# A graph network on one core: the zero fill, the attention table and the edge tables moved out of the preparation

## The chip, the cores and the metric

The kernel runs on one core of a Trainium2 chip. A core has a matrix engine (PE, whose weight loads are listed apart as PEld), a vector engine (DVE), an activation engine (ACT), GpSimd (POOL), and SyncE (SP), which here only issues transfers. Each engine takes its instructions in order from its own queue and waits at semaphores for the others. Transfers are issued from the queues of SP, ACT and POOL and carried by 16 DMA engines.

The metric is the device time of one execution in microseconds (us), as a median of several runs. Beside it stands one execution taken by the hardware profiler, with its span (first to last instruction).

## The reference

A graph of 12,500 nodes and 400,000 edges, sorted by destination; each node has 32 features. Four layers follow one another, each as `x = layernorm(x + layer(x))`:

```python
x = _layernorm(x + _L0_gnn_ref(x, src, dst, w1_W, w1_b, w2_W, w2_b, a))   # attention over the sources
x = _layernorm(x + _L1_gnn_ref(x, edge_index, 3))                         # three rounds of means
x = _layernorm(x + _L2_gnn_ref(x, edge_index, edge_attr_32, W1, b1, W2, b2))  # edge network, maximum
x = _layernorm(x + _L3_gnn_ref(x, edge_index))                            # three rounds of normed sums
```

L0 weighs the sources of a node by a softmax of `a . w2(x_dst - x_src)`. Within one destination the part of `x_dst` cancels, so each source has one weight, `exp(logit - maximum)`, which can be put into a table once. L1 and L3 sum the rows of the sources for each destination. L2 runs a small network over every edge and takes the maximum for each destination; it needs, edge by edge, the row of the source and the row of the destination.

## The kernel before

**A.** The kernel writes the graph down as a dense matrix A of small counts, one byte for each pair of nodes: 25 chunks of 512 destinations, each against 98 groups of 128 sources. Sums over edges then are matmuls of A with a table of node rows, split into three bf16 parts (`split`, `x3`).

**Preparation (lines 395 to 617).** `zero` is memset and written to all of `starts_d` (50 MB, line 429, on ACT's queue); it is needed in the edge layer. `code` and `srcs` (1.6 MB each) are loaded, a word is packed for each edge and stored to `code_d`. `firsts` holds the destination of every 128th edge. 25 comparisons (`mk`, line 460) with matmuls count them into `row`, which goes out to `row_d` and comes back as `row_i`; 25 gathers fetch these rows of `dst`, and `lt` and `ws` (lines 493 to 497) give the first edge of each window of four destinations. `ws` goes out to `ws_d`. Then comes `attention_table` (line 335): for each of 25 groups of four, PE transposes of `X`, an ACT copy to `xT`, matmuls with `wc`, and three DVE operations into `ex`, `lg` and `X`; at the end the extremes of `lg`, an exponential, a product over all of `ex` and `split` into `x3`. Then come the edge layer's tables (lines 504 to 560): in six pieces, `dsh` and `rw` are loaded, DVE makes `rows_d`, the flags `cont_d` (two stores) and the heads of three stages. Then `ws` is read back (line 567), counts and the list of overflowing windows are made (lines 563 to 617, 803 to 821).

**Build (lines 620 to 850).** Windows are the rows of a chunk. `runs(q)` says how many runs of 128 edges chunk q has for each of its 128 windows: 4, 3, 2 or 1. What does not fit goes to an extra chunk `Ax` of at most 128 rows of 512 edges, handled first (c = -1, four runs). For each chunk `chunk_keys` gathers the words `g` from `code_d`; `edge_keys` unpacks them (`ki`, line 643) to `pl`. `build_half` makes one-hots on DVE, `ol` (line 706) and `oh` (line 711), from the pool `hot`, one pair for each run in each of eight steps; PE multiplies them (line 721, `pa`), ACT copies to `at` (line 727), SP stores `at` to A (line 732). Between these matmuls `go_on(4)` takes steps from the list `steps`: generators that multiply a finished half by `x3` (`multiply`, line 741) and finish a chunk of the attention layer (`attend`).

**L1 (lines 879 to 906).** Three rounds of `R.product`: for each chunk SP loads A in two tiles `a` (line 314, three buffers), PE multiplies them (line 318), and DVE checks the counts with `top` (line 325), one quarter of A in each round. Then follow the edge layer and L3.

**Order.** A scheduler interleaves the instructions of each engine's queue when the program is built; it follows the data and the buffers, so code written later may stand earlier in a queue.

Of the kernel before, what the change touches and what calls it, by code (L numbers as in the profile page):

```python
# [8 lines left out]
F32 = mybir.dt.float32  # L9
F16 = mybir.dt.float16  # L10
BF16 = mybir.dt.bfloat16
# [11 lines left out]
P = 128  # L23
# [28 lines left out]
def runs(q):  # L52

    return 4 if q == 0 else 3 if q == 1 else 2 if q < 9 else 1
# [60 lines left out]
def dense_path(ctx, tc, bad_i, x, src, dst, edge_attr, w1T, w1_b, w2, w2T, w2_b, aT,  # L115
# [140 lines left out]
    class Rounds:  # L256
        def __init__(self, st, x3s=2):
            self.x3p = st.enter_context(tc.tile_pool(name="x3p", bufs=x3s))
            self.wk = st.enter_context(tc.tile_pool(name="wk", bufs=2))
            self.one = st.enter_context(tc.tile_pool(name="one", bufs=1))  # L260
# [72 lines left out]
    def attention_table(R, t0):  # L333

        lg = R.one.tile([P, H], F32, name="lg")
        x3 = R.new_x3()
        with tc.tile_pool(name="l0", bufs=1) as l0, \
                tc.tile_pool(name="l0p", bufs=1, space=PSUM) as l0p, \  # L340
                tc.tile_pool(name="l0y", bufs=3, space=PSUM) as l0y:
            pu = l0p.tile([P, P], F32, name="pu")
            nc.tensor.matmul(pu[:D, 0:1], w2_sb, a_sb, start=True, stop=True)
            nc.vector.memset(wc[D:, D:D + 1], 0.0)
            nc.vector.tensor_scalar_mul(wc[:D, D:D + 1], pu[:D, 0:1], -1.0)
            xT = [l0.tile([D + 1, 4, P], F32, name=f"xT{i}") for i in range(2)]
            for t in xT:
                nc.vector.memset(t[D:], 1.0)
            for n_, h0 in enumerate(range(0, H, 4)):
                k = min(4, H - h0)  # L350
                pT = l0y.tile([P, 4, P], F32, name="y")
                for j in range(k):
                    nc.tensor.transpose(pT[:D, j, :], X[:, h0 + j, :], ident)
                nc.scalar.copy(xT[n_ % 2][:D, :k], pT[:D, :k])
                pm = l0y.tile([P, 4, P], F32, name="y")
                for j in range(k):
                    nc.tensor.matmul(pm[:, j, :2 * D + 1], xT[n_ % 2][:, j, :], wc,
                                     start=True, stop=True)
                nc.vector.tensor_copy(t0[:, h0:h0 + k, :D], pm[:, :k, :D])
                nc.vector.tensor_copy(lg[:, h0:h0 + k], pm[:, :k, D])  # L360
                nc.vector.tensor_add(X[:, h0:h0 + k, :], X[:, h0:h0 + k, :],
                                     pm[:, :k, D + 1:2 * D + 1])

            mm = l0.tile([P, 2], F32, name="mm")
            nc.vector.reduce_max(mm[:, 0:1], lg, axis=AX.X)
            nc.vector.tensor_reduce(mm[:, 1:2], lg, axis=AX.X, op=OP.min)
            nc.vector.tensor_scalar_mul(mm[:, 1:2], mm[:, 1:2], -1.0)
            pu = l0p.tile([P, P], F32, name="pu")
            nc.tensor.transpose(pu[:2, :], mm, ident)
            ext = l0.tile([2, 1], F32, name="ext")  # L370
            nc.vector.reduce_max(ext, pu[:2, :], axis=AX.X)
            pick = l0.tile([2, 2], F32, name="pick")
            nc.vector.tensor_scalar(pick, ident[:2, :2], ext, None, op0=OP.mult)
            pu = l0p.tile([P, P], F32, name="pu")
            nc.tensor.matmul(pu[:, :2], ones[:2, :], pick, start=True, stop=True)
            gm = l0.tile([P, 2], F32, name="gm")
            nc.vector.tensor_copy(gm, pu[:, :2])
            wide = l0.tile([P, 1], F32, name="wide")
            nc.vector.tensor_add(wide, gm[:, 0:1], gm[:, 1:2])
            fits = l0.tile([P, 1], F32, name="fits")  # L380
            nc.vector.tensor_scalar(fits, wide, SPAN, None, op0=OP.is_le)
            nc.vector.tensor_sub(more, more, fits)
            nc.vector.tensor_scalar_add(more, more, 1.0)
            nc.vector.tensor_scalar_mul(gm, gm, -1.0)
            nc.scalar.activation(t0[:, :, D], lg, AF.Exp, bias=gm[:, 0:1])
            nc.vector.tensor_mul(t0[:, :, :D], t0[:, :, :D], over(t0[:, :, D], H))
            nc.vector.memset(t0[:, :, D + 1], 1.0)
            for h0 in range(0, H, 14):
                split(R.wk, x3, t0[:, h0:h0 + 14, :], h0, 14, F0)
        return x3  # L390
# [4 lines left out]
    with ExitStack() as build:  # L395
# [29 lines left out]
        with tc.tile_pool(name="prep", bufs=1) as prep, \  # L425
                tc.tile_pool(name="prep2", bufs=2) as prep2:
            zero = prep.tile([P, 25 * D], F32, name="zero")
            nc.vector.memset(zero, 0.0)
            nc.scalar.dma_start(starts_d[:E].rearrange("(p b t) d -> p b (t d)", p=P, t=25),
                                zero[:, None, :].to_broadcast([P, C // 25, 25 * D]))  # L430
# [59 lines left out]
            x3 = attention_table(R, ex)  # L490

# [10 lines left out]


        with tc.tile_pool(name="e_prep", bufs=2) as prep:
            CP = -(-C // 5)
            d0 = keys.tile([P, 1], F32, name="d0")
            run = keys.tile([P, 1], F32, name="run")
            for s in range(len(HS) + 1):
                e0, Cs = P * cuts[s], cuts[s + 1] - cuts[s]

                def view(ap):
                    return ap[e0:e0 + P * Cs].rearrange("(p t) -> p t", p=P)

                cont0, single, fix, first_row = heads[s]
                nc.gpsimd.iota(run, pattern=[[0, 1]], base=e0 - 1, channel_multiplier=Cs,
                               allow_small_or_imprecise_dtypes=True)
                pieces = -(-Cs // CP)
                size = -(-Cs // pieces)
                for c0 in range(0, Cs, size):
                    n = min(size, Cs - c0)  # L520
                    sl = slice(c0, c0 + n)
                    dsh = prep.tile([P, CP + 1], I32, name="dsh")[:, :n + 1]
                    if e0 or c0:
                        nc.sync.dma_start(dsh, bass.AP(tensor=dst.tensor,
                                                       offset=dst.offset + e0 + c0 - 1,
                                                       ap=[[Cs, P], [1, n + 1]]))
                    else:
                        nc.vector.memset(dsh[:, 0:1], -1)
                        nc.sync.dma_start(dsh[:, 1:], view(dst)[:, sl])
                        nc.sync.dma_start(dsh[1:, 0:1], bass.AP(tensor=dst.tensor,  # L530
                                                                offset=dst.offset + Cs - 1,
                                                                ap=[[Cs, P - 1], [1, 1]]))
                    rw = prep.tile([P, CP], I32, name="rw")[:, :n]
                    nc.sync.dma_start(rw, view(src)[:, sl])
                    lo = prep.tile([P, CP], I32, name="lo")[:, :n]
                    hi = prep.tile([P, CP], I32, name="hi")[:, :n]
                    table_row(rw, rw, lo, hi)
                    nc.sync.dma_start(view(rows_d)[:, sl], rw)
                    t = prep.tile([P, CP], F32, name="t")[:, :n]
                    acc = prep.tile([P, 1], F32, name="acc")  # L540
                    nc.vector.tensor_tensor(t, dsh[:, 1:], dsh[:, :n], op=OP.is_lt)
                    nc.vector.reduce_sum(acc, t, axis=AX.X)
                    nc.vector.tensor_add(more, more, acc)
                    cont = prep.tile([P, CP], F32, name="cont")[:, :n]
                    nc.vector.tensor_tensor(cont, dsh[:, 1:], dsh[:, :n], op=OP.is_equal)
                    nc.sync.dma_start(view(cont_d[0])[:, sl], cont)
                    contb = prep.tile([P, CP], F32, name="contb")[:, :n]
                    nc.vector.tensor_scalar(contb, cont, -0.5, BIG, op0=OP.add, op1=OP.mult)
                    nc.vector.tensor_scalar_mul(contb, contb, 2.0)
                    nc.sync.dma_start(view(cont_d[1])[:, sl], contb)  # L550
                    if c0 == 0:
                        nc.vector.tensor_copy(cont0, cont[:, 0:1])
                        nc.vector.tensor_copy(d0, dsh[:, 1:2])
                        table_row(first_row, dsh[:, 1:2], lo[:, 0:1], hi[:, 0:1])
                    nc.vector.tensor_scalar(t, dsh[:, 1:], d0, None, op0=OP.is_equal)
# [1407 lines left out]
```

## Time and profile before

| what | us |
|---|---|
| median of three runs (11362.96 to 11370.98) | 11369.12 |
| the profiled execution | 8876.0 |
| its span | 8873.8 |
| preparation, to the first one-hot `oh` | 352.9 |
| build of A with the attention layer, to the last product at 1681 | about 1330 |
| L1, from its first matmul at 1696.6 to about 3414 | about 1717 |
| edge layer, to about 7519 | about 4105 |
| L3, to the end | about 1355 |

The profiled execution is 2493 us shorter than the median of the runs; its mean granted PE clock is 0.785. Busy over the span: PE 87%, PEld 53%, DVE 51%, ACT 18%, POOL 37%. Such shares are means over stages that have different limits, so the stages are read one by one: a digit in the page's slices is the busy share of an engine in tenths, a timeline row gives when an instruction started and who ended the idle time before it.

### The profile page before, as it was taken

Reading aid. Unit: us, or ns where it says so; the run is one execution under the profiler, and the core shown is the slowest. Engines: PE = TensorE matmul, PEld = TensorE weight load, DVE = VectorE, ACT = ScalarE, POOL = GpSimd, SP = SyncE. Lnnn points to the kernel's source line nnn. Section 1 sums busy time; section 2 is a strip of 40 time slices with the busy share of each in tenths; the row PEclk is TensorE's granted clock in tenths of the full one; section 3 lists DMA queues with packets and bytes.
Section 4 is the critical chain, followed back from the end, with each engine's and each line's share of the span. In section 5 each row is a group of like instructions: output and inputs, shape, how many; then the busy total and the mean of one; then the engine's idle time right before and its main releaser. Section 6 shows DMA issues by size and latency. Waiting matters only on the chain.

```text
span 8873.8 us, 98544 instructions
## 1 busy us (share of the span) xinstructions
PE 7726.1 (87%) x38282; PEld 4718.2 (53%) x38282; DVE 4490.1 (51%) x9484; ACT 1623.5 (18%) x3211; POOL 3302.1 (37%) x3398
## 2 busy tenths in 40 slices
PE   2678899999999997688888888888869958999999
PEld 1468899755656554333433433443325635655655
DVE  2799988666666774333333333333333333366211
ACT  0224577400000001111111111111112211100000
POOL 1001110000000115777777777777777774000000
PEclk8689999999999997555555555555558969999999
DMA  7112244577777774222222122222226726777776
GB/s 273 49 60 112 119 172 176 232 286 286 284 290 286 292 292 148 57 54 55 51 54 57 50 56 54 53 54 52 56 52 201 249 69 204 266 289 286 283 288 240
DMA packets 442397, 1439.34 MB, mean 162 GB/s; under 512 B 115551, under 2 KB 200863, under 8 KB 428351
## 3 DMA queue, kind: packets, MB, share of 16 engines
q1 hardware_dynamic: 312864, 1317.77, 39.8%
q0 software_dynamic: 108576, 60.70, 4.1%
q10 hardware_dynamic: 20480, 54.47, 1.6%
q8 instruction: 304, 4.98, 0.2%
q14 instruction: 173, 1.42, 0.1%
HBM read 1155.20 MB, written 277.47 MB: 161 GB/s over the span
## 4 chain that ended last, share of the span: by engine, by line
PE 47%; POOL 27%; issue 9%; DVE 4%; DMA 3%; ACT 1%; POOLq 0%; ACTq 0%; DVEq 0%; SPq 0%
PE y L318 32%; POOL ef L105 26%; PE y L741 3%; PE y L987 3%; DMA ef<-table,rows 3%; DVE oh L711 2%; PE z L253 2%; PE pa L721 2%; DVE ol L706 1%; PE pv L1294 1%; PE ph L1276 1%; POOL ends L105 1%; PE pT L1247 1%; PE y L247 1%; PE ph L1278 1%
## 5 line engine op out<-in xcount | busy, mean ns | idle before, releaser
L105 POOL DMA_INDIRECT ef<-table,rows x3125 | 2953.3, 945 | 952.1 <-issue 922.9
L318 PE MATMUL y<-a,x 128*96 128x512 fp8e4 (+1 forms) x13338 | 2886.2, 376 | 21.7 <-DMA a<-Ax 21.7
L318 PEld LDWEIGHTS <-x 128*96 128x96 bf16 x13338 | 1627.4, 124 | 1161.0 <-issue 16.3
L1249 DVE COPY eT<-pT 96x512 f32<-96x512 f32 x782 | 535.8, 685 | 2362.2 <-PE pT L1247 2350.2
L325 DVE TENSOR_REDUCE top<-a 128x1 f32<-128x6272 uint8 x204 | 1363.6, 6685 | 658.0 <-DMA a<-A 636.4
L1247 PE MATMUL pT<-ident,ef 128*96 128x128 f32 x3125 | 1139.4, 411 | 518.3 <-DMA ef<-table,rows 489.5
L1247 PEld LDWEIGHTS pT<-ident,ef 128*96 128x96 f32 x3125 | 546.1, 186 | 1495.2 <-DMA ef<-table,rows 919.9
L1276 PE MATMUL ph<-eT,mw 96*64 96x256 f32 x1564 | 807.7, 616 | 91.2 <-DVE eT L1249 72.9
L1294 PE MATMUL pv<-mw,hT 128*128 128x64 f32 x3124 | 803.4, 398 | 89.8 <-ACT hT L1281 81.8
L1294 PEld LDWEIGHTS pv<-mw,hT 128*128 128x128 f32 x3124 | 695.3, 302 | 345.4 <-ACT hT L1281 202.2
L721 PE MATMUL pa<-oh,ol 128*128 128x196 bf16 x5184 | 715.8, 263 | 119.7 <-DVE oh L711 69.3
L1278 PE MATMUL ph<-eT,mw 96*64 96x256 f32 x1562 | 808.1, 617 | 0.0
L727 ACT ACTIVATE at<-pa 128x784 uint16<-128x784 f32 x816 | 651.2, 823 | 552.2 <-PE pa L721 527.9
L1281 ACT ACTIVATE hT<-ph,mb 128x256 f32<-128x256 f32 x781 | 370.5, 474 | 2072.8 <-PE ph L1278 2065.3
L741 PE MATMUL y<-at,x 128*102 128x256 fp8e4 x4998 | 724.6, 274 | 22.1 <-ACT at L727 22.1
L110 POOL DMA_INDIRECT starts_d<-X,start_i x98 | 95.0, 969 | 1645.0 <-DVE X L228 1622.5
L721 PEld LDWEIGHTS <-ol 128*128 128x128 bf16 x5184 | 544.2, 118 | 165.6 <-issue 108.7
L711 DVE TENSOR_TENSOR oh<-bins_h,pl 128x1568 bf16<-128x1568 bf16 x648 | 626.0, 966 | 0.0
L741 PEld LDWEIGHTS <-x 128*102 128x102 bf16 x4998 | 545.5, 126 | 40.1 <-issue 30.8
L706 DVE TENSOR_TENSOR ol<-la,lb 128x512 bf16<-128x512 bf16 x1296 | 491.1, 418 | 75.6 <-PE pa L721 75.1
L105 POOL DMA_INDIRECT g<-code_d,ws_i x25 | 119.0, 4760 | 1006.7 <-DVE ki L643 1006.7
L987 PE MATMUL y<-a,x 128*96 128x512 fp8e4 (+1 forms) x1950 | 492.5, 390 | 0.9 <-DVE x L241 0.9
(298 smaller groups left out, 4088.8 us busy)
## 6 DMA issues: line engine op xcount, KB each, us to landing
a<-A SPq DMA_DIRECT2D x240, 3136.0 KB
A<-at SPq DMA_DIRECT2D x98, 1568.0 KB
a<-A SPq DMA_DIRECT2D x48, 1152.0 KB
starts_d<-zero ACTq DMA_DIRECT2D x1, 50000.0 KB
ef<-table,rows POOLq DMA_INDIRECT x3125
attr<-in_edge_attr SPq DMA_DIRECT2D x63, 768.0 KB
begin<-starts_d SPq DMA_DIRECT2D x63, 768.0 KB
scan<-o SPq DMA_DIRECT2D x63, 768.0 KB
```

The source lines that it names most:

```text
L105: return nc.gpsimd.indirect_dma_start(out=o, out_offset=None, in_=tab, in_offset=IndirectOffsetOnAxis(ap=idx, axis=0))
L318: nc.tensor.matmul(y[:3 * F, :nq * Q], x3[:, h, :3 * F], a[:, :nq, h - h0, :], start=(h == first), stop=(c < 0 and h == H - 1))
L325: nc.vector.reduce_max(top[:, col:col + 1], a[:, quarter].bitcast(U8).rearrange("p h c -> p (h c)"), axis=AX.X)
L711: nc.vector.tensor_tensor(oh, bins_h[:, None].to_broadcast([P, 4, HJ, 2]), pairs(pl[:, t, 0, half * 64 + w0:half * 64 + w0 + 8])[:, :, Non ...
L721: nc.tensor.matmul(pa[:, 2 * b + i, :HJ], ols[t][:, u, :, :, 2 * b + i].rearrange("p a b -> p (a b)"), ohs[t][:, 2 * u + b, :, i], start=( ...
L727: nc.scalar.activation(at[:, qd, :, off:off + 8].rearrange("p h (w j) -> p h w j", w=4), pa[:, :, :HJ].rearrange("p w (h j) -> p h w j", h ...
L741: nc.tensor.matmul(y[:3 * F0, half * 2 * Q:(half + 1) * 2 * Q], x3[:, h, :3 * F0], at[:, :, h, :], start=(h == 0), stop=(c < 0 and h == H ...
L987: nc.tensor.matmul(y[:3 * D, :nq * Q], x3[:, h, :3 * D], a[:, :nq, h - h0, :], start=(h == lo), stop=(h == hi - 1))
L1247: nc.tensor.transpose(pT[:3 * D, j, :], B.ef[:, t + j, :], ident)
L1276: nc.tensor.matmul(ph[:HID, :ka], mw1, eT[:, :ka], start=True, stop=True)
L1278: nc.tensor.matmul(ph[HID:2 * HID, :k - 2], mw1, eT[:, 2:k], start=True, stop=True)
L1294: nc.tensor.matmul(pv[:, j].rearrange("p h d -> p (h d)"), hT[:, j, :], mw2, start=True, stop=True)
```

## The change

- The zero fill is no longer first. `zero` is made from the first keys (`pl` of the extra chunk, times 0.0), and the store to `starts_d` is issued on ACT's queue after them.
- `attention_table` becomes the generator `attention`, put first on `steps`, so that its parts are taken by `go_on` in the build of the extra chunk. Its PSUM tiles come from the build's pools `p_y` (two buffers) and `p_z`, its `xT` from `ys`. The product over `ex` is made in seven parts. `multiply` takes its PSUM tile when it begins.
- The edge layer's tables become the function `edge_tables`, called after L1's first round.
- The pool `hot` has five buffers for each of `ol` and `oh` instead of six.
- `runs(q)` is 2 up to q = 6 instead of q = 8.

```diff
-    return 4 if q == 0 else 3 if q == 1 else 2 if q < 9 else 1
+    return 4 if q == 0 else 3 if q == 1 else 2 if q < 7 else 1
...
-    def attention_table(R, t0):
...
+    def attention(x3, t0, lg, p_y, p_z):
...
+        def part2(n_, h0, k):
+            pm = p_y.tile([P, CH], F32, name="y0").rearrange("p (k e) -> p k e", e=P)
+            for j in range(k):
+                nc.tensor.matmul(pm[:, j, :2 * D + 1], xT[n_ % 2][:D + 1, j, :], wc,
+                                 start=True, stop=True)
+            late.append((h0, k, pm))
+
+        def part3(h0, k, pm):
+            nc.vector.tensor_copy(t0[:, h0:h0 + k, :D], pm[:, :k, :D])
+            nc.vector.tensor_copy(lg[:, h0:h0 + k], pm[:, :k, D])
+            nc.vector.tensor_add(X[:, h0:h0 + k, :], X[:, h0:h0 + k, :],
+                                 pm[:, :k, D + 1:2 * D + 1])
+
+        for n_, h0 in enumerate(range(0, H, 4)):
+            k = min(4, H - h0)
+            pT = p_y.tile([P, CH], F32, name="y0").rearrange("p (k e) -> p k e", e=P)
+            for j in range(k):
+                nc.tensor.transpose(pT[:D, j, :], X[:, h0 + j, :], ident)
+            nc.scalar.copy(xT[n_ % 2][:D, :k], pT[:D, :k])
+            yield
+            part2(n_, h0, k)
+            yield
+            yield
+            part3(*late.pop(0))
+            yield
...
+        for h0 in range(0, H, 14):
+            sl = slice(h0, h0 + 14)
+            nc.vector.tensor_mul(t0[:, sl, :D], t0[:, sl, :D], over(t0[:, sl, D], 14))
+            nc.vector.memset(t0[:, sl, D + 1], 1.0)
+            split(wk, x3, t0[:, sl, :], h0, 14, F0)
+            yield
+
+    def edge_tables():
...
-            zero = prep.tile([P, 25 * D], F32, name="zero")
-            nc.vector.memset(zero, 0.0)
-            nc.scalar.dma_start(starts_d[:E].rearrange("(p b t) d -> p b (t d)", p=P, t=25),
-                                zero[:, None, :].to_broadcast([P, C // 25, 25 * D]))
...
-            x3 = attention_table(R, ex)
...
-        hot = build.enter_context(tc.tile_pool(name="hot", bufs=6))
+        hot = build.enter_context(tc.tile_pool(name="hot", bufs=5))
...
+        x3 = R.new_x3()
+        lg = keys.tile([P, H], F32, name="lg")
...
         def multiply(at, y, c, half, last, done):
+            if half == 0:
+                y.append(p_y.tile([P, CH], F32, name="y0"))
+            y = y[0]
...
+        nc.vector.tensor_scalar_mul(
+            zero.bitcast(BF16), todo[0][0].rearrange("p t m w -> p (t m w)")[:, :2 * 25 * D], 0.0)
+        nc.scalar.dma_start(starts_d[:E].rearrange("(p b t) d -> p b (t d)", p=P, t=25),
+                            zero[:, None, :].to_broadcast([P, C // 25, 25 * D]))
...
+        steps.append(attention(x3, ex, lg, p_y, p_z))
         for c in range(-1, NQ):
             pl, n, to, halves, done = todo.pop(0)
-            y = p_y.tile([P, CH], F32, name="y0")
+            y = []
...
             R.product(x3, post1, r)
+            if r == 0:
+                edge_tables()
```

## The prediction

> **What bounds the kernel now.** I read first the page's forty slices, each about 222 us wide:
>
> ```profile
> PE   2678899999999997688888888888869958999999
> DVE  2799988666666774333333333333333333366211
> PEclk8689999999999997555555555555558969999999
> DMA  7112244577777774222222122222226726777776
> ```
>
> No engine is full in slices 0 and 1, the preparation. Slices 1 to 7 build A, 7 to 15 are L1, 15 to 33 the edge layer, 33 to 39 L3. The change touches the preparation, the build and the start of L1, so the timeline of the first 360 us comes next (start, duration, engine, line, operation; in brackets the idle time before it and who ended it):
>
> ```profile
> 2.43 0.65 ACTq L429 DMA_DIRECT2D starts_d<-zero  x1
> 4.68 34.95 SPq L434 DMA_DIRECT2D code<-in_dst  x1
> 86.89 0.18 DVE L449 CAST first_f<-firsts 128x25 f32<-128x25 int32 x1 [63.33 <-DMA firsts<-in_dst]
> 130.20 3.48 DVE L465 TENSOR_SCALAR row<-pr 1x3200 int32<-1x3200 f32 x1 [1.65 <-PE pr L463]
> 151.56 0.23 SPq L467 DMA_DIRECT2D row_d<-row  x1
> 191.71 3.49 DVE L493 TENSOR_TENSOR lt<-rows,w 128x3200 f32<-128x3200 int32 x1 [57.53 <-DMA rows<-in_dst,row_i]
> 214.14 0.06 DVE L528 MEMSET dsh<- 128x1 int32 x1 [14.98 <-DMA ws_d<-ws]
> ...
> 327.81 0.66 DVE L578 MEMSET cap<- 128x1 f32 x25 [0.59 <-DMA cont_d<-contb]
> ...
> 352.86 0.97 DVE L711 TENSOR_TENSOR oh<-bins_h,pl 128x1568 bf16<-128x1568 bf16 x1
> ```
>
> It is a chain of waits. The zero fill (50 MB) is issued at 2.4 us and keeps the transfers near 395 GB/s until about 151; `firsts`, 12 KB, arrives only at 86.9. The row marks last until 133.7; the store of `row` leaves 18 us after it is ready; the gathers end at 191.7; the store of the window starts lands at 214.1. Only then do the attention groups run on (3.65 us each, to 298), the edge tables between and after them, and A's first one-hot starts at 352.9.
>
> Then the build, by windows (from:to, length, busy us and count of PE, PEld, DVE, ACT, POOL, granted clock, DMA share, GB/s), and the gathers of keys, one for each chunk of A:
>
> ```profile
> 400.00:500.00 100.00, 78.11 (x666) 70.34 (x665) 97.24 (x197) 24.71 (x31) 0.94 (x1) 0.88 0.13 51
> 900.00:1000.00 100.00, 91.27 (x878) 84.69 (x877) 100.00 (x205) 50.62 (x67) 10.07 (x2) 1.00 0.28 115
> 1300.00:1400.00 100.00, 96.69 (x930) 93.91 (x930) 85.38 (x182) 74.61 (x99) 1.91 (x2) 0.98 0.43 179
> ```
>
> ```profile
> 766.99 9.32 POOL L105 DMA_INDIRECT g<-code_d,ws_i  x1 [47.07 <-DVE ki L643]
> 823.38 9.34 POOL L105 DMA_INDIRECT g<-code_d,ws_i  x1 [47.06 <-DVE ki L643]
> ...
> 1322.19 0.95 POOL L105 DMA_INDIRECT g<-code_d,ws_i  x1 [35.64 <-DVE ki L643]
> 1358.78 0.96 POOL L105 DMA_INDIRECT g<-code_d,ws_i  x1 [35.65 <-DVE ki L643]
> ```
>
> Up to about 1100 DVE, making one-hots, is the bound; after it PE. A chunk of two runs takes 823.4 - 767.0 = **56.4 us**, one of a single run 1358.8 - 1322.2 = **36.6 us**. L1 is PE's: 22.4 us a chunk, DVE at 65%.
>
> **The change, part by part.**
>
> *Fill moved, to the first one-hot (new 0 to 75 us).* `X`, `code` and `srcs`, 1.6 MB each, need 12 us at 395 GB/s. X comes in 128-byte rows: `row_i`, 3200 single words, landed in 4.1 us, and the last gather needed 2.1 (issue over at 189.6, `lt` at 191.7), so 3200 pieces cost about 2; I allow some 8 us for X's 12,500 rows, and 4 for `firsts`. Behind the issues at 4.7 us this gives `first_f` at about 28 instead of 86.9. Bounds: 20 (`srcs` was used at 16.5 even beside the fill) and 45. The marks keep their 47 us (86.9 to 133.7): `row` at 75, and its store leaves at once, since the fill is no longer in its way.
>
> *Attention as steps.* From `row` on the old durations apply: 3 us to `row_i`, 4.1 to the first gather, 33 to `lt`: 115. But in the new program's DVE queue twelve attention groups stand ahead of `lt`: 75 + 12 x 3.65 + 3 = 122. `lt` and `ws` take 7, groups between them about 1: 130. The store of `ws` takes its 15 (198.98 to 214.14): 145. Reading it back to `n` took 5.8: 151. Now PE's queue decides: the product of `xn` stands behind the seventeenth group, two groups are mixed with the 25 small products (8 us: 160), four more (4 x 3.65) stand ahead of the first key product: 175, and keys to one-hots take 5: **180**. Thus 352.9 - 180 = **173 us** earlier. This counts the fill, the tables and the attention together; what is late next is the attention groups themselves, still in this chain. Were they not in it, the keys would be there at 115 + 7 + 15 + 25 (327.8 to 352.9) = 162.
>
> The attention's end, in the build now: multiplying `ex` 3.4, L239 4.3, L241 4.3, the small ones 1.7, two late groups 1.4; with the zeroing from the keys (1600 elements, half a `mk` of 3200 at 1.05) 15.6 us on a DVE that is full. About half lands in waits made by the next part: **+8**.
>
> *Five buffers of `hot` instead of six.* With four runs (16 steps in the extra chunk, 16 in chunk 0) a step makes four pairs of `ol` and `oh`, 1.56 us each. PE finishes 2.57 us after the last pair at full clock (441.81 to the second copy at 444.38), 4.49 at the lower one (448.04 to 452.53). With six buffers DVE has two pairs, 3.12 us, before it needs one back; with five only 1.56. So it waits 1.0 us in a fast step and 1.5 more than now in a slow one. The clock averaged 0.85 from 350 to 700, so about 10 of 32 are slow: 22 x 1.0 + 10 x 1.5 = **+37**. With three or fewer runs two pairs remain free: about 0.
>
> Here the Trainium skill speaks against the change (TensorE: Matmul & The Clock Gate, "HAM oscillation"): gaps over some 3.4 us send PE back to half clock. In the wait list of 352 to 1110 PE's longest gap for `oh` is 2.0 us and the clock is already low at times; 1.0 more stays under 3.4. By the rule, if every step falls to the low clock, it is 32 x 2.9 = 93 us; by the rows 37. I take the rows, and keep 93 as the upper end (lower: 10, nearly all filled by other DVE work).
>
> *Two runs only up to q = 6.* Chunks 7 and 8 go to one run: 2 x (56.4 - 36.6) = **-40**. What no longer fits goes to the extra chunk, whose size is fixed; counted from the inputs, its rows in use rise from 80 to 96 of 128, so the general path stays out.
>
> *The fill beside the build.* From 183 us, 50 MB at 395 GB/s are 127 us. A half of `at` (two writes of 1.57 MB, 4 us each alone) is made every 56 us and has two buffers; the next keys are gathered a chunk ahead. Hidden: 0; uncovered, at most 127. Chunk 0's keys are asked for just before it.
>
> *Edge tables beside L1.* Six pieces, 6.4 us of DVE each: 38 us, over some 25 tiles of A, where DVE is idle about 3.6 us in each 11.2. On SP's queue some 31 small transfers, several waiting for DVE, stand between the loads of A. A load of A lands about 11 us ahead of its use, and has three buffers. POOL's three `run` values have nothing behind them until the scatter of the last round. I take **+3**, bounds 0 and 40.
>
> Sum: -173 + 8 + 37 - 40 + 3 = **-165 us**, a span of 8709 in place of 8873.8, an execution of 8711 in place of 8876.0. The runs' median is 11369, 2493 above this execution; no view here shows where these lie. Waits for transfers and DVE work should keep their size there, so I subtract the same: **11204**.
>
> **Rivals.**
> 1. *Attention stays wholly in the way.* For: PE and DVE keep their order, so each late arrival stops both chains. Then only the fill's 75 us and the tables' 25 (302 to 327) go: -100 + 8 + 37 - 40 + 3 = -92: 11277. Against: group and main chain use different resources most of the time.
> 2. *A larger gain.* `firsts` at 20, the attention hidden (first one-hot 154), waits filled (10): -199 + 10 - 40 = -229: 11140. For: DVE is nearly empty before. Against: PE's order.
> 3. *Slower: SP's queue in L1.* A transfer at its head that waits for DVE, which itself waits for the load of A behind it in time, starves PE. Price: 26 loads of A lie among the tables' transfers; each that comes t later than its 11 us of slack costs t. Without my +3 the sum is -168, so it decides from t = 6.5 us; at 8 it is +40: 11409. For: the queue is in order, and a table's load lands behind 3.1 MB of A. Against: DVE runs a tile ahead of PE.
> 4. *The change doesn't do what it says:* the fill takes the engines' turns from A's writes, and DVE waits for `at`; the 127 us come back: -38: 11331.
>
> **How the numbers follow.** Forecast, -110 to -225: 0.60. Rival 1, 0.13; rival 2, 0.14; rival 4, 0.04; no change 0.03; rival 3, 0.06. A measurement tells 0.2% (23 us) from no change: faster 0.91, same 0.03, slower 0.06. From the bounds (`firsts` 20 to 45, buffers 10 to 93, L1 up to 40) and most of rivals 1 and 2: 11100 to 11310.
>
> **What would show it.** First one-hot near 180, `first_f` near 28; DVE waits on PE's `pa` of about 1 us a step in the four-run chunks; seven gathers of keys 56 us apart becoming five; no idle PE in L1 for `a`. I am wrong if the first one-hot is later than 230, if PE waits for A in L1's first two rounds, or if the clock in the four-run chunks falls to 0.5.

## The result, and the profile after

The kernel after takes 11210.1 us (11208.1 to 11216.2), the kernel before, beside it on the same chip, 11368.4: a ratio of **0.9862, with an interval of 0.9845 to 0.9879**, 158 us less. The forecast was 11204, 165 less. The profiled execution of after took 11211.6 us, its span is 11209.0, its mean granted PE clock 0.719. Some series of executions, of either kernel, run the edge layer some 2300 us slower than others (the profiled execution of before was a short one), so times are compared only with those of before in the same series, and stages only between traces of one kind.

The forty slices of after, each now 280 us wide:

```profile
PE   5789999999963455555445555445444564689999
DVE  5898877666742222222222222222232112236511
PEclk6899999999985555555555555555556775799999
DMA  4324467777751111111111111111112442467776
```

Slice 0 has PE at 5 and DVE at 5 where before had 2 and 2. Its slice is the wider one, but the first 222 us alone agree: PE is busy for 127.6 us of them (48.5 before), DVE for 101.9 (65.9). The edge layer (slices 12 to 34) leaves every engine idle for about half of the time or more (PE is busy 50% of it, the others less): that is the longer kind, not the change, as E1 and E0 show. The timeline of the preparation of after:

```profile
26.95 0.18 DVE L522 CAST first_f<-firsts 128x25 f32<-128x25 int32 x1 [8.78 <-DMA firsts<-in_dst]
...
75.26 0.23 SPq L540 DMA_DIRECT2D row_d<-row  x1
...
99.33 0.29 DVE L359 COPY ex<-y 128x128 f32<-128x128 f32 x1 [8.63 <-remote]
...
116.18 0.29 DVE L359 COPY ex<-y 128x128 f32<-128x128 f32 x1 [16.30 <-remote]
...
137.66 3.48 DVE L564 TENSOR_TENSOR lt<-rows,w 128x3200 f32<-128x3200 int32 x1
...
161.73 0.71 DVE L590 MEMSET cap<- 128x1 f32 x24 [16.03 <-issue]
...
168.47 0.19 DVE L581 TENSOR_TENSOR n<-n,ws 128x25 f32<-128x25 f32 x1 [0.34 <-DMA n<-ws_d]
...
202.16 0.97 DVE L726 TENSOR_TENSOR oh<-bins_h,pl 128x1568 bf16<-128x1568 bf16 x1
```

`first_f` moved from 86.9 to 27.0 and the store of `row` from 151.6 to 75.3, as forecast. Then two attention groups wait 8.6 and 16.3 us for a "remote" releaser, an event whose sender the trace doesn't name, and `lt`, queued behind them, starts at 137.7. `cap` stands still for 16.0 us behind the store of `ws`; E10 asks what that costs. The first one-hot comes at 202.2 instead of 352.9.

The build of the two four-run chunks (`c = -1` and chunk 0), half by half: windows with the busy time of PE, PEld, DVE, ACT and POOL, then granted clock, DMA share and GB/s. First before, then after:

```profile
353.00:423.30 70.30, 48.65 (x357) 41.55 (x358) 66.78 (x138) 16.17 (x21) 0.94 (x1) 0.77 0.14 53
423.30:480.90 57.60, 42.21 (x352) 36.95 (x351) 55.84 (x111) 16.48 (x21) 0.00 (x0) 0.85 0.08 32
480.90:545.00 64.10, 49.56 (x401) 44.82 (x400) 59.14 (x127) 16.83 (x23) 1.82 (x1) 0.84 0.17 70
545.00:602.40 57.40, 43.32 (x330) 37.77 (x329) 54.19 (x106) 13.12 (x16) 0.00 (x0) 0.82 0.08 35
```

```profile
202.60:300.90 98.30, 61.37 (x366) 50.47 (x366) 81.84 (x179) 26.55 (x42) 4.57 (x1) 0.64 0.96 385
300.90:368.00 67.10, 48.49 (x351) 41.62 (x350) 57.42 (x120) 14.25 (x18) 9.46 (x2) 0.73 0.70 281
368.00:434.90 66.90, 49.80 (x384) 44.20 (x383) 59.48 (x127) 16.11 (x22) 1.89 (x2) 0.81 0.13 53
434.90:498.90 64.00, 44.85 (x350) 39.38 (x349) 54.31 (x106) 13.20 (x17) 0.00 (x0) 0.81 0.12 51
```

Every half became longer, the first by 28 us. There DVE has 15 us more work and 13 us more idle time (98.3 - 81.8 = 16.5 against 70.3 - 66.8 = 3.5). In the others its work is the same within 2 us and the idle time grows. DMA is at 0.96 and 0.70 in the first two: the fill.

Stage by stage, read from the starts of the first, 129th, 177th and last `oh`, of L1's first matmul and of the first gather of the edge layer. E1 (before) and E0 (after) are the kernels unchanged, profiled once more, described below; each column subtracts two traces of one kind:

| stage | E1 to after | before to E0 | forecast |
|---|---|---|---|
| to the first one-hot | 357.5 to 202.2: -155.3 | 352.9 to 183.3: -169.6 | -173 |
| four runs, 128 one-hots | 252.3 to 296.3: +44.0 | 249.3 to 297.6: +48.3 | +45 |
| three runs, 48 one-hots | 82.6 to 83.0: +0.4 | 82.6 to 83.0: +0.5 | 0 |
| two and one runs, to the last one-hot | 971.6 to 924.5: -47.1 | 971.9 to 926.4: -45.5 | -40 |
| last one-hot | 1664.0 to 1506.0: -158.0 | 1656.6 to 1490.4: -166.2 | -168 |
| L1, to the first gather of the edge layer | 1732.0 to 1731.8: -0.1 | 1731.6 to 1731.6: 0.0 | +3 |

Of the wait that L1 was feared to get, nothing shows. PE's idle time behind loads of A, over all rounds of L1 and L3, on the page of after:

```profile
L317 PE MATMUL y<-a,x 128*96 128x512 fp8e4 (+1 forms) x13338 | 2887.3, 376 | 24.0 <-DMA a<-Ax 24.0
```

Before it was 21.7. In L1 there is one such wait, at its start: 12.3 us, and 11.9 before. So the gain is made before the last one-hot, and nothing is given back afterwards.

### The profile page after: what moved, and what is told of

It is laid out like the page before. It is cut to its first block, busy times and chain, and to the rows that moved or that the text cites. A ratio compares the mean times of both kernels' runs of the same rounds, so it can differ in the third digit from the quotient of the medians.

```text
span 11209.0 us, 97869 instructions
## 1 busy us (share of the span) xinstructions
PE 7678.3 (69%) x38014; PEld 4722.9 (42%) x38014; DVE 4434.1 (40%) x9388; ACT 1619.4 (14%) x3209; POOL 3284.6 (29%) x3398
## 5 line engine op out<-in xcount | busy, mean ns | idle before, releaser
L317 PE MATMUL y<-a,x 128*96 128x512 fp8e4 (+1 forms) x13338 | 2887.3, 376 | 24.0 <-DMA a<-Ax 24.0
L1273 PE MATMUL pT<-ident,ef 128*96 128x128 f32 x3125 | 1036.4, 408 | 48.2 <-DVE ef L1166 20.9
L1013 PE MATMUL y<-a,x 128*96 128x512 fp8e4 (+1 forms) x1950 | 527.8, 403 | 108.2 <-issue 106.3
L726 DVE TENSOR_TENSOR oh<-bins_h,pl 128x1568 bf16<-128x1568 bf16 x616 | 595.5, 967 | 0.0
L110 POOL DMA_INDIRECT starts_d<-X,start_i x98 | 95.2, 971 | 1428.6 <-DVE X L228 1406.1
L721 DVE TENSOR_TENSOR ol<-la,lb 128x512 bf16<-128x512 bf16 x1232 | 467.4, 418 | 105.9 <-PE pa L736 105.6
L1322 ACT COPY v<-pv 128x128 f32<-128x128 f32 x781 | 207.6, 266 | 2070.9 <-remote 1236.2
```

The lines of the kernel that those rows point to most:

```text
L317: nc.tensor.matmul(y[:3 * F, :nq * Q], x3[:, h, :3 * F], a[:, :nq, h - h0, :], start=(h == first), stop=(c < 0 and h == H - 1))
L726: nc.vector.tensor_tensor(oh, bins_h[:, None].to_broadcast([P, 4, HJ, 2]), pairs(pl[:, t, 0, half * 64 + w0:half * 64 + w0 + 8])[:, :, Non ...
L1273: nc.tensor.transpose(pT[:3 * D, j, :], B.ef[:, t + j, :], ident)
```

## The experiments

Each line of the summary gives the time beside the kernel before in the same series. The last column is the start of the last `oh`, the end of what the change touches but for L1; it resolves a few us, where a time resolves some 15.

| run | time | before | ratio (interval) | first / last one-hot |
|---|---|---|---|---|
| E1 before again | 11265.5 (one execution) | 11266.0 | - | 357.5 / 1664.0 |
| E0 after again | 8709.9 | 8879.6 | 0.9808 (0.9794 to 0.9821) | 183.3 / 1490.4 |
| E2 fill in front | 11180.8 | 11266.0 | 0.9920 (0.9906 to 0.9933) | 254.3 / 1571.7 |
| E3 tables in front | 8736.5 | 8882.8 | 0.9837 (0.9824 to 0.9850) | 217.5 / 1519.6 |
| E5 two runs to q = 8 | 11161.1 | 11266.0 | 0.9904 (0.9888 to 0.9919) | 201.9 / 1555.8 |
| E6 before, five buffers | 8899.4 | 8882.8 | 1.0021 (1.0013 to 1.0029) | 354.0 / 1681.6 |
| E7 six buffers | 11096.0 | 11266.0 | 0.9847 (0.9834 to 0.9861) | 202.7 / 1481.7 |
| E8 attention held back | 8723.8 | 8879.6 | 0.9824 (0.9811 to 0.9837) | 173.0 / 1502.7 |
| E10 six buffers, early `cap` | 8690.2 | 8879.6 | 0.9784 (0.9771 to 0.9798) | 183.4 / 1465.5 |
| E12 E10 and E8 | 8700.5 | 8879.6 | 0.9799 (0.9786 to 0.9813) | 172.3 / 1476.6 |
| E13 E10, `mark_last` later | 8683.2 | 8882.8 | **0.9776** (0.9763 to 0.9790) | 181.8 / 1457.3 |
| E15 E13, attention at once | 11104.5 | 11283.5 | 0.9844 (0.9831 to 0.9858) | 211.4 / 1471.3 |

### E1 and E0: the two kernels again

No edit.

> The kernel before, unchanged, profiled once more, so that its stages can be set beside those of the kernel after in the same mode of the edge layer. Theory: the 2493 us between its profiled execution (8876) and its median (11369) lie in the edge layer alone; if this execution is a common one (about 11370), preparation, build, L1 and L3 keep their lengths to 1 per cent (first one-hot 353, last one-hot about 1657) and the edge layer takes about 6400 to 6600 us instead of 4105, with gaps on the vector engine behind semaphores named remote, as in the kernel after. Rival: the 2493 us are spread over all stages, and the first one-hot and the last one come later too, in proportion (about 450 and 2120).

> The kernel after, unchanged, in the same series as the next three, so that small differences are taken on one chip. Every theory: 1.2 to 1.6 per cent under the kernel before.

E1 took 11265.5 us, and the theory holds: preparation and build are within 8 us of the profile before (first one-hot 357.5, last one 1664.0), L1 is the same to 0.3 us, and from the first to the last gather of `ef` 6297.3 us went by (3436.0 to 9733.3) where the profiled execution of before took 4007.3 (3428.2 to 7435.5). That is 2290 of the 2389 us between the two spans; of the rest, 92 lie behind the last gather and 8 ahead of L1. On the page the row that carries it is the vector engine's copy of `eT` (busy us, mean ns, idle time before it and what ended most of it), in E1 and then in the profile before:

```profile
L1249 DVE COPY eT<-pT 96x512 f32<-96x512 f32 x782 | 536.0, 686 | 4711.3 <-remote 1685.7
```

```profile
L1249 DVE COPY eT<-pT 96x512 f32<-96x512 f32 x782 | 535.8, 685 | 2362.2 <-PE pT L1247 2350.2
```

The work is equal to the microsecond; only what it waits for differs. The kind does not go with the chip: one chip ran E1, E2, E5 and E7, of the longer kind, and later E0, E8, E10 and E12, of the short one. E0 turned out to be of the short kind, after as before (8709.9 against 8879.6), and saves 170 us. Its ratio differs from the first one, 0.9862, mostly since 8880 is a smaller whole; the rest is in its preparation:

```profile
119.92 3.48 DVE L564 TENSOR_TENSOR lt<-rows,w 128x3200 f32<-128x3200 int32 x1
...
149.68 0.18 DVE L581 TENSOR_TENSOR n<-n,ws 128x25 f32<-128x25 f32 x1 [0.56 <-DMA n<-ws_d]
...
183.33 0.97 DVE L726 TENSOR_TENSOR oh<-bins_h,pl 128x1568 bf16<-128x1568 bf16 x1
```

The same program, in the same order, without a remote wait: `lt` at 119.9 (forecast 122), `n` at 149.7 (151), the first one-hot at 183.3 (180). So 19 of the 22 us by which after's profile missed 180 come with those waits, not from the order of the work: 17.7 of the 18.8 us between the two traces are there at `lt` already.

### E2: the zero fill alone put back

```diff
+            zero = prep.tile([P, 25 * D], F32, name="zero")
+            nc.vector.memset(zero, 0.0)
+            nc.scalar.dma_start(starts_d[:E]...)
...
-        nc.vector.tensor_scalar_mul(zero.bitcast(BF16), todo[0][0]..., 0.0)
-        nc.scalar.dma_start(starts_d[:E]...)
```

> The kernel after, with the zero fill put back to the front of the preparation (memset and store as in the kernel before), all else as after. Theory: the fill holds up the first loads; first_f falls back from 27 to about 87 and the first one-hot from 202 to 262 to 275, so the time rises by 60 to 75 us over the kernel after (11270 to 11285). Rival: attention and tables were the chain and the fill was hidden beside them; the time rises by less than 20 us.

The ratio rises from 0.9862 to 0.9920, some 65 us of 11266; the last one-hot comes 65.7 us later than in after. The timeline shows the old wait again, and where part of it arises: issuing `code`, just ahead of `firsts` on SP's queue, keeps that queue for 34.9 us. In after (the single row) it takes 14.4.

```profile
4.69 34.94 SPq L511 DMA_DIRECT2D code<-in_dst  x1
...
87.69 0.18 DVE L526 CAST first_f<-firsts 128x25 f32<-128x25 int32 x1 [64.13 <-DMA firsts<-in_dst]
...
254.34 0.97 DVE L729 TENSOR_TENSOR oh<-bins_h,pl 128x1568 bf16<-128x1568 bf16 x1
```

```profile
4.69 14.41 SPq L507 DMA_DIRECT2D code<-in_dst  x1
```

The first one-hot loses 52.1 us, less than the 60.7 that `first_f` loses and less than expected. The remote waits can explain it: after has them in this kind of series, and E2 has none before its first one-hot, since no attention group runs there before 217. Against E0, which has none either, the first one-hot is 71.0 us later; that comparison is across two kinds of series. More is lost in the build: the attention's groups (`ex` from `y`) run from 217 to 332 us here, against 79 to 217 in after, so more of them fall into the extra chunk, whose first half lasts 109.3 us against 98.3. The rival, under 20 us, falls. And the build gains nothing by being rid of the fill: the second half of the extra chunk takes 67.0 us at a DMA share of 0.07, against 67.1 at 0.70 in after. The fill really is covered there.

### E3: the tables alone put back

```diff
+        edge_tables()
+
         with tc.tile_pool(name="prep3", bufs=1) as prep, \
...
-            if r == 0:
-                edge_tables()
```

> The kernel after, with the edge layer's tables back in the preparation: edge_tables is called ahead of the reading back of ws, not behind L1's first round. Theory: the six pieces (about 38 us of the vector engine, and their loads and stores) lie again partly between ws and n and beside the attention groups; the first one-hot comes 15 to 30 us later, L1 gains 0 to 3 us back, and the last one-hot is 12 to 30 us later than in the kernel after. Rival: without the fill in their way the tables fit into the waits of the preparation: less than 8 us later, and their move was worth nothing.

First one-hot 34.2 us later than in E0, a little more than expected, last one 29.2; the ratio goes from 0.9808 to 0.9837, about 26 us. The timeline shows where:

```profile
180.53 0.74 DVE L592 MEMSET cap<- 128x1 f32 x25 [0.22 <-DMA cont_d<-contb]
...
186.76 0.19 DVE L583 TENSOR_TENSOR n<-n,ws 128x25 f32<-128x25 f32 x1 [1.79 <-DMA n<-ws_d]
...
217.46 0.97 DVE L728 TENSOR_TENSOR oh<-bins_h,pl 128x1568 bf16<-128x1568 bf16 x1
```

`n`, 149.7 in E0, is at 186.8: the pieces of the tables stand between `ws` and its reading back. Moving them beside L1 was worth what the forecast's first rival had given the tables (25 us), and cost L1 nothing.

### E5: two runs up to chunk 8 again

```diff
-    return 4 if q == 0 else 3 if q == 1 else 2 if q < 7 else 1
+    return 4 if q == 0 else 3 if q == 1 else 2 if q < 9 else 1
```

> The kernel after, with two runs up to chunk 8 again, as before. Theory: chunks 7 and 8 cost a two-run chunk instead of a one-run one, 2 x (56.4 - 36.6) = 40 us by the trace of before, 47 by the difference of the two traces over the two- and one-run stages: 11250 to 11257. Rival: the two-run stage gained by something else (the fill gone, attention gone), and undoing the runs gives less than 25 us.

The last one-hot is 49.8 us later than in after, all of it in this stage: two runs take 406.0 us instead of 285.8, and the one-run chunks behind them 568.3 instead of 638.7. The ratio rises by 0.0042, 47 us. So by the difference of the stages the two chunks cost 60.1 us each with two runs ((406.0 - 285.8) / 2) and 35.2 with one ((638.7 - 568.3) / 2), not 56.4 and 36.6. The kernel before had it in its means: seven two-run chunks in 405.5 us and sixteen of one run in 566.3 are 57.9 and 35.4 each, 45 us for two chunks. The gathers of keys in after show why one interval was a poor sample:

```profile
662.74 9.32 POOL L105 DMA_INDIRECT g<-code_d,ws_i  x1 [246.01 <-DVE ki L657]
719.13 9.33 POOL L105 DMA_INDIRECT g<-code_d,ws_i  x1 [47.06 <-DVE ki L657]
783.03 9.33 POOL L105 DMA_INDIRECT g<-code_d,ws_i  x1 [54.58 <-DVE ki L657]
839.03 9.33 POOL L105 DMA_INDIRECT g<-code_d,ws_i  x1 [46.67 <-DVE ki L657]
```

Successive starts are 56.4, 63.9 and 56.0 us apart: in the longer one DVE also has the attention layer's finishing steps (727 to 742 us, among them eight operations of 0.6 to 0.7 us).

### E6 and E7: the sixth buffer, from both sides

```diff
-        hot = build.enter_context(tc.tile_pool(name="hot", bufs=6))
+        hot = build.enter_context(tc.tile_pool(name="hot", bufs=5))
```

This is all of E6, on the kernel before. E7 is after with `bufs=6`; to make room, the zeros lie in `nxt`:

```diff
-        zero = keys.tile([P, 25 * D], F32, name="zero")
...
+        zero_b = nxt.rearrange("p h f -> p (h f)")[:, :2 * 25 * D]
+        zero = zero_b.bitcast(F32)
```

> The kernel before, with hot at five buffers instead of six, nothing else. Theory: the price of the buffer, without the attention's end in the build: 23 us by the four-run stage of the version of after with six buffers (296 to 274), all of it in the two four-run chunks (249 to 272), the three-run chunk and later ones unchanged; the kernel before gets 0.2 to 0.3 per cent slower. Rival: the prediction's 37 us (1.0 us in a fast step, 1.5 in a slow one), stage at 283 or more; or, with no attention to share the vector engine, less than 10.

> The kernel after with six buffers of hot instead of five; to make room, the zeros of the fill are made in the second table x3, which is written only later, instead of in a tile of their own. Theory: in the two four-run chunks the vector engine waits about 1 us a step less on pa: 37 us by the prediction's sum, 11165 to 11180; the four-run stage falls from 296 to about 260. Rival: those 47 us come from the attention's end and its groups in the build, and six buffers gain less than 15 us.

Both give the same price, by the length of the four-run stage: 271.4 in E6 against 249.3 before, **22.1 us**; 273.6 in E7 against 296.3 in after, **22.7**. In E6 the times agree (17 us, 11 to 26); in E7 they are compared across two series, 0.9847 against 0.9862, and that says only that the gain is small. The forecast's 37 is too large, and the expectation for E7 (36 us less in the stage, a time of 11165 to 11180 in a series that ran at another level) misses. What DVE waited for over the first 280 us of the build, in us, times and longest, in the kernel before and then in E6:

```profile
DVE ol L706 <- PE pa L721: 9.9, 15, 0.9
```

```profile
DVE ol L706 <- PE pa L721: 33.6, 23, 2.5
```

The difference, 23.7 us, is the price. It does not come as 1 us in each of 32 steps: DVE waits 23 times, 1.5 us each, and 15 times, 0.7 us each, before.

The halves of E6, to be set beside those of the kernel before above:

```profile
354.00:426.80 72.80, 47.18 (x354) 41.06 (x355) 66.99 (x141) 19.41 (x26) 5.43 (x1) 0.78 0.08 32
426.80:493.80 67.00, 46.95 (x347) 40.49 (x345) 57.38 (x121) 13.99 (x18) 9.87 (x2) 0.78 0.12 48
493.80:560.60 66.80, 49.69 (x385) 44.17 (x384) 59.50 (x128) 16.08 (x22) 1.89 (x2) 0.81 0.13 53
560.60:625.30 64.70, 46.25 (x350) 39.95 (x349) 54.16 (x106) 12.95 (x16) 0.00 (x0) 0.76 0.12 51
```

The price lies in the second and the fourth half (+9.4 and +7.3 us), little in the first and the third (+2.5 and +2.7). The last three halves of after are as long as these within 1 us, so there the missing sixth buffer explains all that after lost. The clock of the last three was 0.85, 0.84 and 0.82 before, and is 0.78, 0.81 and 0.76 here. Had every step fallen to half clock, it would have shown near 0.5.

### E8 and E12: the attention groups held back

```diff
-        nc.vector.memset(wc[D:, D:D + 1], 0.0)
+        nc.vector.tensor_scalar_mul(wc[D:, D:D + 1], gate, 0.0)
...
-        steps.append(attention(x3, ex, lg, p_y, p_z))
+        steps.append(attention(x3, ex, lg, p_y, p_z, ws_i[D:D + 1, 0:1]))
```

E12 is the same on top of E10.

> The kernel after, with the attention groups held back: the column of wc that all of them need is made from ws_i (times 0.0) instead of a memset, so they can begin only when ws_i is there, behind the gathers of rows. Theory: the 22 us that the first one-hot came later than forecast are 16 us at lt (the groups ahead of it on the vector engine stand still while GpSimd issues the 25 gathers) and 6 behind n; with the groups away lt falls from 138 to 113 to 118 and the first one-hot from 202 to 168 to 180. The groups then load the extra chunk: its first half grows from 98 us to 105 to 125, and the time is 0 to 25 us under the kernel after. Rival: the gathers themselves land late, or the store of ws sets the pace whatever stands ahead: lt at 130 or later, first one-hot at 195 or later, and the time is not below the kernel after.

> Six buffers, cap set at the start, and the attention groups held back until ws_i, all together. Theory: the parts add: 23 us for the buffers, 0 to 25 for the groups, so 25 to 50 us under the kernel after, first one-hot at 165 to 178. Rival: with the groups in the extra chunk TensorE becomes its bound, and all that comes earlier is given back: no more than the six buffers alone (15 to 25 us).

Half of it came true. In E8 `lt` starts at 111.9 and the first one-hot at 173.0, 10.3 us earlier than in E0 (this series had no remote waits to take away, so it can't test them). But the first half of the extra chunk grows from 100.2 to 126.2 us, and the last one-hot is 12.3 us later, the time 14 us longer. The first half in E0 and in E8:

```profile
183.30:283.50 100.20, 63.66 (x354) 52.28 (x354) 82.01 (x179) 26.52 (x41) 4.13 (x1) 0.60 0.96 384
```

```profile
173.00:299.10 126.10, 86.96 (x526) 72.19 (x526) 89.78 (x224) 35.18 (x55) 0.94 (x1) 0.65 0.97 385
```

E12 shows it again: 11.1 us later than E10 at the last one-hot, and 9 us under E0 in time instead of 25 to 50. So its rival came true. Fourteen of the 25 groups went into the build (9 instead of 23 stand ahead of the first one-hot). Out of the preparation, where DVE and PE wait anyway, they gained 10.3 us; in the build they cost 26, with 7.8 us more work on DVE and 23.3 on PE. The order in after, groups first and the key chain a little delayed, is the better one.

### E10 and E13: what the attention costs in the build

E10 is E7 and:

```diff
         ends_x = keys.tile([P, NQ], F32, name="ends_x")
+        cap = keys.tile([P, NQ], F32, name="cap")
+        for q in range(NQ):
+            nc.vector.memset(cap[:, q:q + 1], float(P * runs(q)))
...
-            cap = prep.tile([P, NQ], F32, name="cap")
-            for q in range(NQ):
-                nc.vector.memset(cap[:, q:q + 1], float(P * runs(q)))
```

E13 is E10 and:

```diff
-                if c < 0 and half == 0:
+                if c < 0 and half == 1:
                     mark_last()
```

> The six buffers again (zeros of the fill made in the second x3), and besides cap is set at the start, in a pool of its own kind, so that its memset no longer stands on the vector engine waiting 16 us for the store of ws with attention groups behind it. Theory: n itself waits for that store, so the first one-hot gains only 3 to 6 us (197 to 200), but four groups more are done before it and the first half of the extra chunk falls from 95 to 85 to 90; in all 8 to 15 us under the version with six buffers alone, 31 to 38 under the kernel after. Rival: the 16 us are in the chain, and the first one-hot falls to 190 or below; or the groups are not what fills the extra chunk, and nothing changes.

> Six buffers and cap set at the start, and besides mark_last (25 products of ends_x and seven comparisons, which mark the last rows of the extra chunk) is called with the second half of the extra chunk, not the first. Theory: of the 27 us by which the first half is longer than before (97 against 70), 15 are the vector engine's work for the attention's end and 12 are idle time made by mark_last, whose 17 us of products stand in TensorE's queue behind the attention's extremes (which wait 7.8 us for the vector engine) while all six pairs of hot are full. With it away the first half falls from 97 to 80 to 87, the second grows by 0 to 6, and the time by 6 to 16 us under the version with six buffers and cap. Rival: the extremes of the attention alone hold up TensorE, or the second half pays all of it: within 4 us.

The early `cap` did nothing: the first one-hot of E10 is at 183.4 (E0: 183.3), and `n` at 149.7 in both. The 16 us before the memset delay nobody, since the store of `ws` holds up `n` as long. What E10 gains over E0, 24.9 us at the last one-hot, is the sixth buffer. But E10 shows the attention's price without the buffer's: its four-run stage takes 275.6 us against 249.3 before, **26.3 us more**, all in the first half (97.0 against 70.3; the second, under the fill at a DMA share of 0.97, is as long as before):

```profile
183.40:280.40 97.00, 59.63 (x354) 49.49 (x354) 81.90 (x179) 26.60 (x41) 4.11 (x1) 0.64 0.96 365
280.40:337.70 57.30, 43.77 (x371) 39.60 (x371) 55.25 (x110) 14.12 (x18) 9.60 (x1) 0.85 0.97 374
```

DVE is busy 81.9 us in the first, 15.1 more. The rest is idle time, and PE's timeline in E10 shows its source:

```profile
208.66 0.77 PE L855 MATMUL pt<-ident,ends_x 128*128 128x128 f32 x2 [7.79 <-DVE mm L380]
...
212.58 2.08 PE L855 MATMUL pt<-ident,ends_x 128*128 128x128 f32 x8 [0.84 <-DVE lastx L857]
215.50 2.08 PE L855 MATMUL pt<-ident,ends_x 128*128 128x128 f32 x8 [0.84 <-DVE lastx L857]
...
224.85 5.03 PE L735 MATMUL pa<-oh,ol 128*128 128x196 bf16 x34
```

PE stands 7.8 us for `mm`, the extremes of the logits, which DVE reaches only behind its one-hots; then come the products of `mark_last`, to 224.9. A set of eight of these products takes 2.08 us here, at a clock of 0.50; in the kernel before it took 1.06 to 1.16, at 0.85. All that time nothing of `pa` is made, the six pairs of `hot` fill up, and DVE runs dry:

```profile
210.00:225.00 15.00, 10.78 (x42) 9.01 (x41) 6.04 (x17) 1.33 (x2) 0.00 (x0) 0.50 1.02 387
```

6.0 us of work in 15. E13 takes `mark_last` away from there. Its two halves of the extra chunk:

```profile
182.00:265.70 83.70, 48.17 (x305) 39.55 (x305) 77.27 (x172) 26.35 (x41) 4.35 (x1) 0.63 0.95 361
265.70:328.10 62.40, 50.62 (x420) 46.30 (x419) 57.92 (x113) 13.87 (x18) 9.36 (x1) 0.84 1.02 395
```

The first is 13.3 us shorter, the second 5.1 longer, the last one-hot 8.2 us earlier: as the theory had it. E13 has the lowest ratio of all, 0.9776, some 0.3% under the kernel after by the ratios (0.9776 / 0.9808), 33 us by the last one-hot. From E10 (0.9784) its time is not told apart; only the stages show the 8 us.

### E15: all of the attention at once

E13, and one line behind `steps.append(attention(...))`:

```diff
+        go_on(10 ** 6)
```

> The version with six buffers, cap at the start and mark_last in the second half, and besides the attention isn't taken step by step in the build: all its steps are taken at once, ahead of the loop over chunks, so the scheduler puts its last groups and the extremes ahead of the first one-hots. Theory: the price of the attention in the build is 15 us of the vector engine plus the 7.3 us in which TensorE waits for mm; with the extremes ahead the wait goes, the first one-hot comes 2 to 9 us later (182 to 184 to 191), the first half falls from 84 to 70 to 78, and the last one-hot is 0 to 8 us earlier than 1457. Rival: the stepping is what hides the attention; without it the first one-hot is 15 us or more later and the last one 8 or more.

It fell into a series of the longer kind, so it can't be set beside E13, only beside E7: first one-hot 8.7 us later, first half 71.6 us instead of 95.2, last one-hot 10.4 us earlier (0.9844 against 0.9847). Its first half:

```profile
211.40:283.00 71.60, 39.37 (x284) 32.31 (x284) 69.45 (x142) 23.93 (x35) 4.10 (x1) 0.69 1.02 391
```

With no attention in it this half is as long as before within 1.3 us although the fill takes a DMA share of 1.02: the fill is covered in the first half as well. E13 had gained 8.2 over E10 by `mark_last` alone. Taking the attention step by step or at once thus makes some 2 us of difference, which these runs don't resolve. The rival (first one-hot 15 us later) falls: the scheduler places the groups in the waits either way, and the generator isn't what hides them.

## Why the prediction was right, and where only its sum was

Its reasons hold; in the four-run stage two of its terms were wrong in opposite directions, and in the total, as measured in the result, two more.

- **First one-hot, -173.** Right in every link. Without remote waits the working came within 4 us at `lt`, `n` and the one-hot (-169.6 in all); with them, as in the result, it is -155.3. That the engines can stand still while gathers are issued wasn't foreseen, and the profile of before, a short execution, couldn't show it. The parts, undone singly, cost 65 us (fill) and 29 us (tables) at the last one-hot. No run puts the attention alone back: its share is known by difference only, some 64 us of the 169.6 at the first one-hot (less 71.0 and 34.2), if the parts add.
- **The attention's end, +8.** Wrong by 18: 26. The 15.6 us of DVE work were sized right (15.1). The failing step is "about half lands in waits made by the next part": the buffer's waits fall in other halves (E6), so all 15 were on the path, and some 11 of idle time came on top: the wait for `mm` and `mark_last` behind it on PE. In the kernel before, `mark_last` was covered by a full DVE (22.0 us busy of the 23 from 400 to 423). E13 shows 7 of the 11 by moving `mark_last` (four-run stage 268.9 instead of 275.6); that the rest is the wait for `mm` is read from E10's timeline only; no run takes it away alone.
- **Five buffers, +37.** Too large: 22. The mechanism (DVE waits for a pair to come free) was right; the count was not. The sum charged a wait in each of 32 steps, and 23 were made. The upper end of 93 took the rule of the Trainium skill (TensorE: Matmul & The Clock Gate, "HAM oscillation") as met in every step. Its gaps of some 3.4 us did not occur: in the last three halves PE's longest wait is 1.2 us, in the kernel before and in E6. The clock fell all the same, but only by 0.03 to 0.07, so the rows were the better guide, and were still too high.
- **Two runs up to q = 6, -40.** -46 to -50: a two-run chunk is 60 us where it was taken from one interval of 56.4, and a one-run chunk 35 where it was taken as 36.6.
- **The fill beside the build, 0.** Right: the second half of the extra chunk lasts 57.3 us in E10 under the fill, 57.6 before without it, and the first 71.6 in E15, 70.3 before.
- **Edge tables beside L1, +3.** 0.0. Rival 3 (loads of A late behind SP's queue) didn't happen.
- **2493 us carried over.** Right, and now located: between the traces of after and E0, one kernel in both kinds, 2499 us of span differ, and 2396 of them lie between the first and the last gather of the edge layer (6403.1 against 4007.5), which the change doesn't touch. Why a series is of one kind or the other stays open.

The sum of +8 and +37 was 45, that of 26 and 22 is 48. The total came out within 2 us at the start of L1 (-166.9 against -168, before to E0) by this cancelling. In the result itself the first one-hot, with its remote waits, gave 18 us less and the two-run chunks 7 more, so that -158 stands beside -165. Both agreements are luck in part, and should not be read as a precision of the method. Of what was to show it wrong, none occurred: the first one-hot is under 230, PE doesn't wait for A more than before, and the clock is at 0.60 or above in every half of after and of E0 (0.50 only for moments, as in the 15 us of E10 shown).

## What to carry to other kernels

A large transfer that nobody needs soon belongs behind the small loads that start a chain, and under a stage that hardly uses the DMA engines: that alone was worth 65 us here. Work taken out of a chain of waits into a stage whose bound is the engine it uses costs its full length there, and more if its products stand in PE's queue ahead of what that engine waits for; ask what idles behind each such wait. Price a buffer by the waits counted in the trace and a chunk by the mean of several, not by one.

## What the runs showed of the hardware

While GpSimd issues gathers back to back (every 1.25 us, 81 to 112), DVE and ACT of one and the same program either go on as ever or stop at semaphores for 8 to 16 us, by the series: the copies of `ex` wait 3.1 us each in E0, and two of them 8.6 and 16.3 in after. In the edge layer the same waits come by the dozen (83 of them, 1685.7 us, before `eT` in E1, none named so in the profile before). The issuing itself is as fast in both (945 and 947 ns a gather). E1 and E2, of the longer kind too, have no such wait in the preparation; there no attention group runs while the 25 gathers are issued. Who sends the missing event, and why only in some series, stays open; no run was made to separate it.

The large store on ACT's queue delays the small loads on SP's in two ways. With the fill in front (E2) SP's queue is held for 34.9 us by issuing the 1.6 MB of `code` (14.4 in after), and from the first issue of `firsts` to its use 48.0 us pass (39.7 to 87.7) instead of 7.8 (19.2 to 27.0).

The granted clock of PE lies below full speed also where PE never waits long: 0.82 to 0.85 in the last three halves before, with no wait over 1.2 us.
